# 13x13 depthwise convolutions on TensorE: column-shifted copies in the contraction, four channels in column tiles, and Toeplitz matrices expanded in DRAM early

## The chip, the cores and the metric

One core of one Trainium2 chip. The metric is the time of one execution on the device, in microseconds. All numbers in tables by stage come from the trace of one profiled execution of each kernel. A kernel that was timed in several rounds has a median and an interval; a kernel that was looked at once has one time, its state is unknown, and it is compared by its stages and not by its total.

## The reference

Four layers on a batch of 8 images, 384 channels of 32x32, fp32. Layer 0 is a norm, a scan in both directions and a gated 3x3 convolution; layer 1 is a convolution block, linear attention and an MLP. The change concerns layers 2 and 3 (cut to what matters):

```python
# layer 2: seven depthwise convolutions, each with its batch norm, summed
out = bn_eval(dwconv(x, w_lk, 1), ...)                     # 13x13
for i, (w, r) in enumerate(zip(branch_ws, (1, 1, 2, 3, 4, 5))):
    out = out + bn_eval(dwconv(x, w, r), ...)              # 5x5 to 3x3, dilated
# layer 3
y = jnp.einsum('bchw,oc->bohw', x, pw_w)                   # pointwise
x_pw = bn(y, ...) + x
out = bn(dwconv(x_pw, dwk_w), ...)                         # 13x13
out = out + bn(x_pw * dw1_w.reshape(1, -1, 1, 1), ...)
return jax.nn.gelu(out, approximate=False)
```

Both layers are one 13x13 depthwise convolution each, once the norms and small kernels are folded into it. So the end of the program is: convolution a, pointwise product, convolution b.

## The kernel before

Image rows lie in the partitions: four channels of 32 rows fill 128 partitions. For each of the 13 column shifts, one product with a 128x128 matrix that holds four 32x32 Toeplitz blocks on its diagonal does all 13 row taps of four channels. Three quarters of that matrix are zero.

```python
x2_d = dram.tile([C, H, B, W], FP, tag="x2_d", name="x2_d")   # input of convolution a
xp_d = dram.tile([C, H, B, W], FP, tag="xp_d", name="xp_d")   # input of convolution b
...
def conv(g_d, src_d, tag, put):
    srcv = src_d.rearrange("(g q) h b w -> g (q h) (b w)", q=4)
    for g in range(NG):                                    # 96 groups of four channels
        if g % GB == 0:
            xt = cxp.tile([P, GB, BW], FP, tag="xt", ...)
            nc.sync.dma_start(xt, srcv[g : g + GB].rearrange("g p n -> p g n"))
        tp = toep[g % NTO]
        for q in range(4):                                 # 32x13x32 windows, 128 B pieces
            one_k = g_d[4 * g + q]
            win = bass.AP(one_k.tensor, one_k.offset, [[1, H], [TG, KS], [1, H]])
            eng = nc.sync if q % 2 == 0 else nc.scalar
            eng.dma_start(tp[q * H : (q + 1) * H, :, q * H : (q + 1) * H], win)
        ...
        for i, kx in enumerate(order):
            s = kx - KS // 2
            lo, hi = _span(s, W)
            nc.tensor.matmul(pv[:, :, lo:hi], tp[:, kx, :], xg[:, :, lo + s : hi + s], ...)
        put(g, ps[:, 0:BW])
...
# pointwise, 16 steps t of two rows of all images
yt = cxp.tile([P, NC, NB], FP, tag="yp", ...)
nc.sync.dma_start(yt, yf[:, :, t * NB : (t + 1) * NB])
...
nc.gpsimd.dma_start(xf[:, :, t * NB : (t + 1) * NB], xo)   # 2 KB pieces
...
# the end of layer 1, image b
nc.gpsimd.dma_start(x2v[m, :, h * (H // 2) : (h + 1) * (H // 2), b, :], o...)  # 128 B pieces
```

## Time and profile before

| stage, by the first product of each (us) | start | length |
|---|---|---|
| layer 0 | 0 | 5215.2 |
| layer 1, to the first product of convolution a | 5215.2 | 2449.7 |
| convolution a | 7664.9 | 496.8 |
| pointwise | 8161.7 | 136.2 |
| convolution b, to the end of the span at 8791.0 | 8297.9 | 493.1 |

The median of four runs is 8790.78 us (8789.93 to 8792.42). The prediction below shows the lines that tell what bounds the convolutions. Two further views matter for what follows. First the DMA issues of the kernel before (written tile, read tensor, queue, count, KB each, median us from issue to landing):

```profile
x_d<-x POOLq DMA_DIRECT2D x48, 256.0 KB, 6.0
...
yp<-y_d SPq DMA_DIRECT2D x16, 768.0 KB, 5.1
xp_d<-xo POOLq DMA_DIRECT2D x16, 768.0 KB, 6.6
out<-ot POOLq DMA_DIRECT2D x96, 128.0 KB, 2.9
```

The pointwise layer's loads (yp) and stores (xp_d) land in 5 to 7 us. `x_d<-x` is the store at the end of layer 1. Both it and `out` write pieces of 128 B. Second, the pointwise stage as a stretch (start and end, us, busy us of PE, PEld, DVE, ACT, POOL with instruction counts, then granted clock, DMA share, GB/s):

```profile
8165.00:8285.00 120.00, 120.00 (x278) 53.07 (x277) 31.83 (x46) 35.74 (x46) 11.44 (x15) 0.99 0.57 182
```

TensorE is busy for all of the 120 us. This stage is bound by TensorE, and DMA is at 0.57.

### The profile page before, as it was taken

Reading aid. Unit: us, or ns where it says so; the run is one execution under the profiler, and the core shown is the slowest. Engines: PE = TensorE matmul, PEld = TensorE weight load, DVE = VectorE, ACT = ScalarE, POOL = GpSimd, SP = SyncE. Lnnn points to the kernel's source line nnn. Section 1 sums busy time; section 2 is a strip of 40 time slices with the busy share of each in tenths; the row PEclk is TensorE's granted clock in tenths of the full one; section 3 lists DMA queues with packets and bytes.
Section 4 is the critical chain, followed back from the end, with each engine's and each line's share of the span. In section 5 each row is a group of like instructions: output and inputs, shape, how many; then the busy total and the mean of one; then the engine's idle time right before and its main releaser. Section 6 shows DMA issues by size and latency. Waiting matters only on the chain.

```text
span 8791.0 us, 45960 instructions
## 1 busy us (share of the span) xinstructions
PE 6984.9 (79%) x17022; PEld 3339.6 (38%) x17022; DVE 4659.7 (53%) x3671; ACT 2213.2 (25%) x2563; POOL 269.2 (3%) x354
## 2 busy tenths in 40 slices
PE   7576676776776766767766679999899998999999
PEld 3132222222222322322322233443444344499599
DVE  2957857867767777677687972342333234100100
ACT  4333233233233233233233211111111111100100
POOL 1000000000000000000000000000000000000011
PEclk8788788788788788778878789999999999999999
DMA  2212111121121121121121220000000000144544
GB/s 69 72 60 67 65 65 65 61 70 64 57 74 64 56 75 64 56 75 64 54 70 68 72 93 11 4 15 15 11 4 15 11 7 4 25 93 95 148 95 86
DMA packets 488852, 492.32 MB, mean 56 GB/s; under 512 B 349212, under 2 KB 378036, under 8 KB 488628
## 3 DMA queue, kind: packets, MB, share of 16 engines
q1 hardware_dynamic: 295220, 382.66, 14.2%
q0 software_dynamic: 24176, 80.14, 3.1%
q10 hardware_dynamic: 169232, 26.58, 1.8%
q8 instruction: 135, 2.21, 0.1%
q14 instruction: 89, 0.73, 0.0%
HBM read 409.15 MB, written 80.11 MB: 56 GB/s over the span
## 4 chain that ended last, share of the span: by engine, by line
PE 37%; issue 32%; DVE 24%; ACT 6%; DMA 1%; POOL 1%; DVEq 0%; POOLq 0%; SPq 0%; ACTq 0%
PE acc L468 10%; DVE hs L463 9%; DVE du L458 5%; PE cv_a L244 5%; PE lc L381 4%; DVE hs L461 4%; PE c L406 4%; DVE hs L466 3%; PE cv_b L244 3%; PE in L360 2%; PE op L484 2%; ACT L435 1%; ACT L436 1%; PE mf L701 1%; PE mo L708 1%
## 5 line engine op out<-in xcount | busy, mean ns | idle before, releaser
L468 PE MATMUL acc<-hs,ident 128*128 128x512 f32 x3072 | 2224.3, 876 | 1369.6 <-DVE hs L466 1369.5
L468 PEld LDWEIGHTS acc<-hs,ident 128*128 128x128 f32 x3072 | 768.5, 269 | 2827.1 <-DVE hs L466 2024.6
L456 ACT ACTIVATE da<-dl,neg_a 128x1024 f32<-128x1024 f32 x768 | 881.1, 1148 | 2478.2 <-DVE hs L461 1298.6
L461 DVE TENSOR_TENSOR_SCAN hs<-da,du 128x1024 f32<-128x1024 f32 x384 | 875.3, 2287 | 169.0 <-PE acc L468 149.1
L466 DVE TENSOR_TENSOR hs<-hs,cc 128x1024 f32<-128x1024 f32 x768 | 919.5, 1215 | 0.4
L458 DVE TENSOR_TENSOR du<-uc,bb 128x1024 f32<-128x1024 f32 x768 | 914.3, 1210 | 0.4
L463 DVE TENSOR_TENSOR_SCAN hs<-da,du 128x1024 f32<-128x1024 f32 x384 | 877.0, 2287 | 4.3 <-PE acc L468 4.2
L701 PE MATMUL mf<-ln,wm 128*128 128x512 f32 x1152 | 562.4, 629 | 78.3 <-DVE ln L695 78.3
L714 DVE SCALAR_TENSOR_TENSOR x<-mo,pk,x 128x512 f32<-128x512 f32 x48 | 36.0, 751 | 1041.8 <-PE mo L708 1038.4
L708 PE MATMUL mo<-hm,wm 128*128 128x512 f32 x1152 | 539.7, 607 | 1.4 <-ACT hm L706 1.4
L244 PE MATMUL cv_b<-xt_b,toep 128*128 128x240 f32 (+6 forms) x2496 | 488.3, 358 | 9.6 <-DMA xt_b<-xp_d 9.6
L244 PE MATMUL cv_a<-xt_a,toep 128*128 128x240 f32 (+6 forms) x2496 | 487.4, 358 | 6.8 <-DMA toep<-g_d 6.8
L244 PEld LDWEIGHTS cv_b<-xt_b,toep 128*128 128x128 f32 x2496 | 466.4, 190 | 31.9 <-issue 10.4
L244 PEld LDWEIGHTS cv_a<-xt_a,toep 128*128 128x128 f32 x2496 | 465.8, 190 | 28.2 <-issue 6.9
L701 PEld LDWEIGHTS mf<-ln,wm 128*128 128x128 f32 x1152 | 232.5, 204 | 382.1 <-issue 282.4
L706 ACT ACTIVATE hm<-mf,biasf 128x512 f32<-128x512 f32 x192 | 131.9, 687 | 951.2 <-PE mf L701 951.2
L381 PE MATMUL lc<-xn,dg 128*128 128x496 f32 (+3 forms) x864 | 356.9, 575 | 0.0
L406 PE MATMUL c<-u,dg 128*128 128x512 f32 (+3 forms) x768 | 334.7, 595 | 5.9 <-ACT dl L434 3.1
L708 PEld LDWEIGHTS mo<-hm,wm 128*128 128x128 f32 x1152 | 205.7, 189 | 328.9 <-issue 199.0
L390 DVE TENSOR_TENSOR lg<-lg,xn 128x512 f32<-128x512 f32 x48 | 33.2, 692 | 496.5 <-ACT lg L389 496.5
L360 PE MATMUL in<-xn,win 128*128 128x512 f32 x576 | 256.4, 603 | 40.4 <-DMA win<-in_inproj_t 26.0
L448 DVE TENSOR_TENSOR uc<-uc,dl 128x1024 f32<-128x1024 f32 x48 | 58.0, 1220 | 398.9 <-PE acc L444 398.7
(153 smaller groups left out, 5628.9 us busy)
## 6 DMA issues: line engine op xcount, KB each, us to landing
bb<-bc_d SPq DMA_DIRECT2D x256, 512.0 KB, 3.6
cc<-bc_d SPq DMA_DIRECT2D x256, 512.0 KB, 3.6
toep<-g_d ACTq DMA_DIRECT2D x384, 52.0 KB, 2.7
toep<-g_d SPq DMA_DIRECT2D x384, 52.0 KB, 2.5
xn<-in_x SPq DMA_DIRECT2D x8, 1536.0 KB, 7.3
xr<-in_x SPq DMA_DIRECT2D x48, 256.0 KB, 3.2
x_d<-lg POOLq DMA_DIRECT2D x48, 256.0 KB, 3.6
fr<-x_d SPq DMA_DIRECT2D x48, 256.0 KB, 2.9
```

The source lines that it names most:

```text
L244: nc.tensor.matmul(pv[:, :, lo:hi], tp[:, kx, :], xg[:, :, lo + s : hi + s], start=(i == 0), stop=(i == KS - 1),)
L360: nc.tensor.matmul(ps, win[:, k, m * P : (m + 1) * P], xn[:, k, bass.ts(h, HALF)], start=(k == 0), stop=(k == NC - 1),)
L381: nc.tensor.matmul(pv[:, ylo - r0 : yhi - r0, xlo:xhi], dg3[:, c, k, :], img[:, ylo + dy : yhi + dy, xlo + dx : xhi + dx], start=(i == 0), ...
L406: nc.tensor.matmul(ps[:, lo - a : hi - a], dg1[:, c, k, :], u[:, c, lo + s : hi + s], start=(i == 0), stop=(i == 3),)
L456: nc.scalar.activation(da, dl[:, c, :], AF.Exp, scale=neg_a[:, c, n : n + 1])
L458: nc.vector.tensor_mul(du, uc[:, c, :], bb)
L461: nc.vector.tensor_tensor_scan(hs, da, du, 0.0, ALU.mult, ALU.add)
L463: nc.vector.tensor_tensor_scan(hs[:, ::-1], da[:, ::-1], du[:, ::-1], 0.0, ALU.mult, ALU.add)
L466: nc.vector.tensor_mul(hs, hs, cc)
L468: nc.tensor.matmul(acc[c][:, bass.ts(h, HALF)], ident, hs[:, bass.ts(h, HALF)], start=False, stop=(d == 1 and n == NST - 1),)
L701: nc.tensor.matmul(ps, wm1[:, k, f * P : (f + 1) * P], xn[:, k, :], start=(k == 0), stop=(k == NC - 1),)
L708: nc.tensor.matmul(acc[m], wm2[:, f, m * P : (m + 1) * P], hm, start=(f == 0), stop=(f == NF - 1),)
```

## The change

The intent: a product that is three quarters zeros wastes TensorE. Now the contraction's 128 partitions hold one channel four times, each copy shifted by one column, so one product does four column shifts, and four products (16 column positions, 13 of them used) make a channel. Each channel's output has 32 rows, so four channels sit side by side in four column tiles of 32. Image rows are stored with zero gaps of six columns between images, so that shifts need no clipping. The Toeplitz matrices are no longer read as windows during the convolution; 128 DMAs from DRAM to DRAM expand them during layer 0, where DMA is mostly idle.

```diff
+KP = 16
+BP = W + KS // 2
+RL = 320
+XL = 316
+CB = 16
...
-    x2_d = dram.tile([C, H, B, W], FP, tag="x2_d", name="x2_d")
+    x2_d = dram.tile([C, H, RL], FP, tag="x2_d", name="x2_d")
-    xp_d = dram.tile([C, H, B, W], FP, tag="xp_d", name="xp_d")
+    xp_d = dram.tile([C, H, RL], FP, tag="xp_d", name="xp_d")
+    e2_d = dram.tile([P, C, 4 * H], FP, tag="e2_d", name="e2_d")
+    e3_d = dram.tile([P, C, 4 * H], FP, tag="e3_d", name="e3_d")
...
+    def side(i, n):                       # called 16 times during layer 0
+        part = C // n
+        for g_d, e_d in ((g2_d, e2_d), (g3_d, e3_d)):
+            for j in range(4):
+                src = g_d[i * part]
+                win = bass.AP(
+                    src.tensor, src.offset + j * TG, [[1, H], [KP * TG, part], [4 * TG, 4], [1, H]]
+                )
+                dst = e_d[j * H : (j + 1) * H, i * part : (i + 1) * part, :]
+                nc.sync.dma_start(dst.rearrange("p c (s o) -> p c s o", o=H), win)
+        ... (zero fills of x2_d and xp_d)
...
+            for c0 in range(0, C, CB):    # convolution, chunks of 16 channels
+                xt = cxp.tile([P, CB, XL], FP, tag="xt", name=f"xt_{tag}_{c0}")
+                for j in range(4):
+                    nc.sync.dma_start(
+                        xt[j * H : (j + 1) * H, :, :],
+                        src_d[c0 : c0 + CB, :, j : j + XL].rearrange("c h n -> h c n"),
+                    )
+                tp = cxp.tile([P, CB, 4, H], FP, tag="tp", name=f"tp_{tag}_{c0}")
+                nc.scalar.dma_start(
+                    tp.rearrange("p c s o -> p c (s o)"), e_d[:, c0 : c0 + CB, :]
+                )
+                for g in range(c0 // 4, (c0 + CB) // 4):
...
+                    for s in range(4):
+                        for q in range(4):
+                            c = 4 * g + q - c0
+                            src = xt[:, c, 4 * s : 4 * s + B * BP].rearrange("p (b n) -> p b n", n=BP)
+                            nc.tensor.matmul(
+                                pv[q * H : (q + 1) * H], tp[:, c, s, :], src[:, :, 0:W],
+                                start=(s == 0), stop=(s == 3),
+                            )
...
-            nc.gpsimd.dma_start(xf[:, :, t * NB : (t + 1) * NB], xo)
+            rows = NB // BW
+            for m in range(NC):
+                for r in range(rows):
+                    nc.gpsimd.dma_start(
+                        xf[m, :, t * rows + r, KS // 2 : KS // 2 + B * BP].rearrange(
+                            "p (b n) -> p b n", n=BP
+                        )[:, :, 0:W],
+                        xo[:, m, r * BW : (r + 1) * BW].rearrange("p (b w) -> p b w", w=W),
+                    )
...
-                        x2v[m, :, h * (H // 2) : (h + 1) * (H // 2), b, :],
+                        x2v[
+                            m, :, h * (H // 2) : (h + 1) * (H // 2),
+                            KS // 2 + BP * b : KS // 2 + BP * b + W,
+                        ],
```

More of the change, by code (lines that the diff above doesn't have):

```diff
@@ L89, in tile_layers @@
     x1_d = dram.tile([B, C, L], FP, tag="x1_d", name="x1_d")
-    x2_d = dram.tile([C, H, B, W], FP, tag="x2_d", name="x2_d")
+    assert KS // 2 + B * BP <= RL and 3 + XL <= RL
+    x2_d = dram.tile([C, H, RL], FP, tag="x2_d", name="x2_d")
     y2_d = dram.tile([C, H, B, W], FP, tag="y2_d", name="y2_d")
-    xp_d = dram.tile([C, H, B, W], FP, tag="xp_d", name="xp_d")
-    g2_d = dram.tile([C, KS, TG], FP, tag="g2_d", name="g2_d")
-    g3_d = dram.tile([C, KS, TG], FP, tag="g3_d", name="g3_d")
+    xp_d = dram.tile([C, H, RL], FP, tag="xp_d", name="xp_d")
+    g2_d = dram.tile([C, KP, TG], FP, tag="g2_d", name="g2_d")
+    g3_d = dram.tile([C, KP, TG], FP, tag="g3_d", name="g3_d")
+    e2_d = dram.tile([P, C, 4 * H], FP, tag="e2_d", name="e2_d")
+    e3_d = dram.tile([P, C, 4 * H], FP, tag="e3_d", name="e3_d")
     bias_d = dram.tile([C], FP, tag="bias_d", name="bias_d")
@@ L154, in tile_layers @@
         nc.scalar.dma_start(k3, dwk.rearrange("(c p) k -> p c k", p=P))
-        g2 = kern.tile([P, NC, KS, TG], FP, tag="g2", name="g2")
+        g2 = kern.tile([P, NC, KP, TG], FP, tag="g2", name="g2")
         nc.gpsimd.memset(g2, 0.0)
-        g3 = kern.tile([P, NC, KS, TG], FP, tag="g3", name="g3")
+        g3 = kern.tile([P, NC, KP, TG], FP, tag="g3", name="g3")
         nc.gpsimd.memset(g3, 0.0)
@@ L175, in tile_layers @@
             src = k3[:, c, :].rearrange("p (a b) -> p a b", b=KS)
-            nc.vector.tensor_scalar_mul(g3[:, c, :, off : off + KS], src, bns("dwk", c))
+            nc.vector.tensor_scalar_mul(g3[:, c, 0:KS, off : off + KS], src, bns("dwk", c))
             mid = g3[:, c, KS // 2, off + KS // 2 : off + KS // 2 + 1]
@@ L185, in tile_layers @@
             nc.gpsimd.dma_start(biasq_d, bias_d.rearrange("(g q) -> q g", q=4))
-    _layer0(tc, nc, B, xv, x1_d, dram, ident, mean_w, eps6, one, vec, neg_a, rs, rsm,
+    zero = const.tile([P, 4 * RL], FP, tag="zero", name="zero")
+    nc.gpsimd.memset(zero, 0.0)
+    def side(i, n):
[8 more added lines that the diff above has]
+                nc.sync.dma_start(dst.rearrange("p c (s o) -> p c s o", o=H), win)
+        rows = H // 8
+        if i % (n // 8) == 0:
+            r = i // (n // 8) * rows
+            for d in (x2_d, xp_d):
+                for c in range(NC):
+                    nc.sync.dma_start(
+                        d[c * P : (c + 1) * P, r : r + rows, :].rearrange("p h n -> p (h n)"), zero
+                    )
+    _layer0(tc, nc, B, xv, x1_d, dram, side, ident, mean_w, eps6, one, vec, neg_a, rs, rsm,
             inproj_t, xproj_t, dtproj_t, outproj_t)
@@ L197, in tile_layers @@
     ) as cps:
-        NTO = 4
-        toep = []
-        for i in range(NTO):
-            t = cwp.tile([P, KS, P], FP, tag=f"toep{i}", name=f"toep{i}")
-            nc.gpsimd.memset(t, 0.0)
-            toep.append(t)
         pwt = cwp.tile([P, NC, C], FP, tag="pwt", name="pwt")
@@ L221, in tile_layers @@
             nc.vector.tensor_add(pbias[:, m, :], pbias[:, m, :], bias2[:, m, :])
-        def conv(g_d, src_d, tag, put):
-            srcv = src_d.rearrange("(g q) h b w -> g (q h) (b w)", q=4)
-            order = [KS // 2] + [i for i in range(KS) if i != KS // 2]
-            xt = None
-            for g in range(NG):
-                if g % GB == 0:
-                    xt = cxp.tile([P, GB, BW], FP, tag="xt", name=f"xt_{tag}_{g}")
-                    nc.sync.dma_start(xt, srcv[g : g + GB].rearrange("g p n -> p g n"))
-                tp = toep[g % NTO]
-                for q in range(4):
-                    one_k = g_d[4 * g + q]
-                    win = bass.AP(one_k.tensor, one_k.offset, [[1, H], [TG, KS], [1, H]])
-                    eng = nc.sync if q % 2 == 0 else nc.scalar
-                    eng.dma_start(tp[q * H : (q + 1) * H, :, q * H : (q + 1) * H], win)
-                ps = cps.tile([P, HALF], FP, tag="cv", name=f"cv_{tag}_{g}")
-                pv = ps[:, 0:BW].rearrange("p (b w) -> p b w", w=W)
-                xg = xt[:, g % GB, :].rearrange("p (b w) -> p b w", w=W)
-                for i, kx in enumerate(order):
-                    s = kx - KS // 2
-                    lo, hi = _span(s, W)
-                    nc.tensor.matmul(
-                        pv[:, :, lo:hi], tp[:, kx, :], xg[:, :, lo + s : hi + s],
-                        start=(i == 0), stop=(i == KS - 1),
-                    )
-                put(g, ps[:, 0:BW])
@@ new lines, in conv @@
+        def conv(e_d, src_d, tag, put):
+            for c0 in range(0, C, CB):
+                xt = cxp.tile([P, CB, XL], FP, tag="xt", name=f"xt_{tag}_{c0}")
+                for j in range(4):
+                    nc.sync.dma_start(
+                        xt[j * H : (j + 1) * H, :, :],
+                        src_d[c0 : c0 + CB, :, j : j + XL].rearrange("c h n -> h c n"),
+                    )
+                tp = cxp.tile([P, CB, 4, H], FP, tag="tp", name=f"tp_{tag}_{c0}")
[3 more added lines that the diff above has]
+                for g in range(c0 // 4, (c0 + CB) // 4):
+                    ps = cps.tile([P, HALF], FP, tag="cv", name=f"cv_{tag}_{g}")
+                    pv = ps[:, 0:BW].rearrange("p (b w) -> p b w", w=W)
+                    for s in range(4):
[6 more added lines that the diff above has]
+                            )
+                    put(g, ps[:, 0:BW])
@@ L261, in put2 @@
                 nc.gpsimd.dma_start(y2v[g - GB + 1 : g + 1].rearrange("g p n -> p g n"), hold["t"])
-        conv(g2_d, x2_d, "a", put2)
+        conv(e2_d, x2_d, "a", put2)
         yf = y2_d.rearrange("(k p) h b w -> p k (h b w)", p=P)
-        xf = xp_d.rearrange("(k p) h b w -> p k (h b w)", p=P)
+        xf = xp_d.rearrange("(k p) h n -> k p h n", p=P)
         NB = min(HALF, H * BW)
@@ L292, in put3, with _layer0 @@
             )
-        conv(g3_d, xp_d, "b", put3)
-def _layer0(tc, nc, B, xv, x1_d, dram, ident, mean_w, eps6, one, vec, neg_a, rs, rsm,
+        conv(e3_d, xp_d, "b", put3)
+def _layer0(tc, nc, B, xv, x1_d, dram, side, ident, mean_w, eps6, one, vec, neg_a, rs, rsm,
             inproj_t, xproj_t, dtproj_t, outproj_t):
@@ L495, in _layer0 @@
             bwd = direction(b, 1, u)
+            side(2 * b, 2 * B)
             scan(b, 0, *fwd, acc)
+            side(2 * b + 1, 2 * B)
             if b + 1 < B:
@@ L515, in _layer1 @@
         x1v = x1_d.rearrange("b (c p) l -> b p c l", p=P)
-        x2v = x2_d.rearrange("(c p) h b w -> c p h b w", p=P)
+        x2v = x2_d.rearrange("(c p) h n -> c p h n", p=P)
         def psum(name):
```

## The prediction

> **What bounds the kernel now.** I read the page first: the slices give the stages. Columns are 40 slices of 220 us; a digit is the busy share in tenths.
>
> ```profile
> PE   7576676776776766767766679999899998999999
> DVE  2957857867767777677687972342333234100100
> PEclk8788788788788788778878789999999999999999
> DMA  2212111121121121121121220000000000144544
> ```
>
> Up to slice 23 (layer 0) DVE and PE share the work, the scan being DVE's; slices 24 to 34 (layer 1) are TensorE; the last five are the two 13x13 convolutions with a pointwise layer between. Only there does DMA reach 4 to 5 tenths. The change speeds up these five slices and puts new transfers into the first 23. Next, the groups of the convolutions, by line (busy us, mean ns, idle before):
>
> ```profile
> L244 PE MATMUL cv_b<-xt_b,toep 128*128 128x240 f32 (+6 forms) x2496 | 488.3, 358 | 9.6 <-DMA xt_b<-xp_d 9.6
> L244 PE MATMUL cv_a<-xt_a,toep 128*128 128x240 f32 (+6 forms) x2496 | 487.4, 358 | 6.8 <-DMA toep<-g_d 6.8
> L244 PEld LDWEIGHTS cv_a<-xt_a,toep 128*128 128x128 f32 x2496 | 465.8, 190 | 28.2 <-issue 6.9
> ```
>
> Each convolution is 487 to 488 us of TensorE with next to no waiting. 96 groups x 13 products are 1248, yet the row counts 2496: an fp32 product is two instructions, each with its own weight load. 487.4 / 2496 is 195 ns start to start (the 358 ns include the pipeline). A group is 26 x 195 ns = 5.08 us; the 13 shifts have 2992 columns together, so a column costs 5.08 us / (2 x 2992) = 0.85 ns per pass. Then the stretches (PE, PEld, DVE, ACT, POOL busy; clock, DMA share, GB/s), in steady convolution and in the steady scan:
>
> ```profile
> 7700.00:8100.00 400.00, 400.00 (x2059) 382.69 (x2059) 16.96 (x40) 14.51 (x39) 15.05 (x20) 1.00 0.45 95
> 2850.00:2990.00 140.00, 93.12 (x112) 35.29 (x112) 124.25 (x83) 30.66 (x28) 0.00 (x0) 0.66 0.22 71
> ```
>
> In the convolution TensorE is busy 400 of 400 us at clock 1.00: **TensorE bound**, DMA under half used. In the scan DVE is busy 124 of 140 us and DMA has 78% to spare. Last, the DMA queues over 7700 to 8100:
>
> ```profile
> q1 hardware_dynamic: 78816, 18.91, 24.5%
> q10 hardware_dynamic: 68256, 8.42, 13.9%
> ```
>
> q10 carries almost only Toeplitz windows in 128 B packets: 13.9% x 16 engines x 400 us / 68256 is 13.0 ns per packet, 9.8 GB/s per engine. In the first 7 us of the pointwise loads (2 KB packets, 128 partitions) I get 20.7 GB/s per engine, and the same (20.8) from the first xt_b loads with 1 KB packets. The only transfer worth reading on 32 partitions is the store of B and C: 0.13 MB, 28.6% of 16 engines in a 2 us window, 14.3 GB/s per engine.
>
> **What the Trainium skill says.** (1) "TensorEngine Tiling (Array Packing)", Tiling Modes: different tiles can load weights and multiply in parallel, four of them at 128x32. No run here shows it yet: every convolution row above is 128*128. (2) "TensorE: Matmul & The Clock Gate", Part 3: three column tiles gave 2.38x; matmuls start and end strictly in order. The trace shows neither. (3) "SBUF — State Buffer", Door 1: partitions 0..31 reach 8 of 16 DMA ports, 189 GB/s at 1 MiB against 328 for all 128. The 14.3 against 20.8 GB/s per engine point the same way (229 against 333 GB/s over 16 engines), on one small store. (4) "DMA: Bandwidth & Descriptors", Specifications: line rate needs 512 B or more. The trace agrees: 9.8 GB/s per engine at 128 B, 20.8 at 1 KB.
>
> **The change, part by part.**
>
> *Convolution, TensorE.* 13 products of 128x128 per group become 16 of 128x32 (4 row-shift blocks x 4 channels, the channels in adjacent column tiles), each over all 256 columns. One pass is 256 x 0.85 = 217 ns. With no overlap of tiles a group is 32 x 217 ns = 6.9 us, worse than 5.08. With ideal overlap of four it would be 1.7 us. I expect between: the two passes of one product use the same tile and come one after the other; in strict order the second pass of channel q can overlap only the first pass of channel q+1, so one channel costs one pass: 16 x 217 ns = **3.5 us per group**, 13.9 us per chunk of 16 channels.
>
> *Convolution, DMA.* Per chunk (24 per convolution): xt is now loaded four times, shifted by one pixel, in four DMAs of 32 partitions x 16 x 1264 B, together 2.59 MB instead of 0.52. At 229 GB/s: 11.3 us. tp is 128 rows of 8 KB, 1.05 MB at 333 GB/s: 3.1 us. The y store, 0.52 MB: 1.6 us. Sum **16.0 us per chunk**, more than TensorE's 13.9. In the second convolution the output store takes the place of y (q0 over 8320 to 8760: 18.2 GB/s per engine, 0.52 MB, 1.8 us): 16.2 us. The 128 B windows, 768 DMAs, are gone from here. The new bound is thus the load of the shifted copies. The order of instructions keeps two chunks of prefetch: the tp load of chunk k+2 stands on ACT's queue right after the evictions of chunk k. Allowing 0.5 us per chunk for imperfect overlap, the convolutions take 24 x 16.5 = 396 and 24 x 16.8 = 403 us: **-91 and -85 us**.
>
> *Starts.* The first chunk needs 2.6 MB instead of 0.5 before the first product: about 11.3 + 2.2 us after issue. Before, it was 9 us for the first convolution and 4 us for the second: **+5 and +10 us**.
>
> *Pointwise layer.* Its output goes out in 96 stores of 1024 pieces of 128 B, not 16 of 2 KB pieces. Such stores exist already (out, same size): 886 ns of POOL each. Six per step are 5.3 us, and a step takes 7.7 us of TensorE (18 instructions x 0.43 us). Hidden: 0.
>
> *Layer 0.* 128 DRAM-to-DRAM DMAs of 3072 pieces of 128 B expand the matrices: at 13 ns on 16 engines 2.5 us each, 320 us in all, and 48 zero fills of 640 KB at 333 GB/s are 2 us each, 94 us. All stand on SP's queue among the loads of B and C. Have these room? From the queue's and DVE's timeline (start, us):
>
> ```profile
> 2883.30 0.32 SPq L451 DMA_DIRECT2D bb<-bc_d  x1
> ```
>
> ```profile
> 2902.39 2.35 DVE L458 TENSOR_TENSOR du<-uc,bb 128x1024 f32<-128x1024 f32 x2
> ```
>
> The product that needs this bb starts 19.1 us after its issue, and bb lands in 3.6: about 15 us of slack. The built order puts mostly one expansion, at times three, or six zero fills, between two loads: 2.5 to 12 us. Mostly hidden; I allow **+20 us** for scan starts, where loads follow B and C directly, and for a somewhat different interleaving.
>
> *Layer 1.* Same stores with another row pitch: 0.
>
> Sum: 8790.5 - 91 - 85 + 5 + 10 + 20 = **8650 us**, 1.6% less.
>
> **The rivals.**
> (a) *Column tiles do not overlap for fp32.* Then TensorE needs 27.7 us per chunk, 665 us per convolution: 2 x 177 more, 9180 us. Against it speaks the skill's 2.38x; for it, that nothing in this trace uses tiles and that fp32 doubles each product. I give it 13%.
> (b) *The loads run at full port rate.* Then 2.59 MB take 7.8 us, a chunk 12.5 us of DMA, and TensorE's 13.9 us bounds it: about 14.3 us per chunk, 343 us per convolution, some 8540 us. For it: 128-partition loads do reach 333, and loads on even and odd ports might overlap. If tiles also overlapped better than I think, DMA at 12.5 would give about 8460. 35% for this direction.
> (c) *The 128 B DRAM-to-DRAM writes are slow.* The 13 ns are from DRAM to SBUF. At 80 ns a DMA would take 15 us, the slack would be gone, and SP, in order, would hold up B and C: hundreds of us in layer 0, 8900 or more. The x2 stores of 128 B pieces (2048 pieces, 6.0 us to landing) argue against more than some 30 ns. 7%.
> (d) *Waiting cools the clock.* With gaps of 2 us per chunk the granted clock could fall as in the scan (0.66) and TensorE would need more than its 13.9 us: up to 18 us per chunk, 8720 us. It lies inside the range.
>
> **Range and chances.** The centre is 8650. The low end, 8510, is (b) with most of its gain; the high end, 8880, is slower loads (18 us per chunk) with 150 us of harm in layer 0. 2% faster means below 8615, only 35 us under the centre, about 1 us per chunk: so faster 0.37. Within 2%, up to 8966: 0.47. Slower, which is (a) or a bad (c): 0.16.
>
> **What would show it right or wrong.** Right: the convolution rows are 128*32, x3072 each; one starts about every 108 ns on average while running; TensorE waits at chunk starts for xt; the DMA digits of the last slices are 8 or 9, at 215 to 230 GB/s; each convolution spans 380 to 420 us; DVE in layer 0 has next to no wait for bb or cc, and layer 1 begins within 40 us of where it did. Wrong: starts 217 ns apart (rival a); xt moving at 300 GB/s (b); DVE waiting for bb after expansions that take over 10 us to land (c); a clock well below 0.9 in the convolutions (d). The prediction fails most easily on the rate of 32-partition loads, which rests on one small store, and on the overlap of tiles, which rests on no run of this case.

## The result, and the profile after

The changed kernel's median is 8759.94 us (four runs, 8755.63 to 8763.78), against 8790.78 us before. The ratio is 0.9965, with a 95% interval of 0.9951 to 0.9979. Ratios here are the mean time of one kernel's fast runs over that of the other's from the same rounds, so not quite the ratio of the medians. A gain of 141 us was forecast, and 31 us came.

By stage, from the traces (us):

| stage | before | after | change | the prediction's terms |
|---|---|---|---|---|
| layer 0 | 5215.2 | 5176.6 | -38.6 | +20 |
| layer 1, to first product of a | 2449.7 | 2465.2 | +15.5 | +5 |
| convolution a | 496.8 | 398.6 | -98.2 | -91 |
| pointwise, to first product of b | 136.2 | 321.8 | **+185.6** | 0 + 10 |
| convolution b, to the end | 493.1 | 398.2 | -94.9 | -85 |
| sum | | | -30.6 | -141 |

The convolutions gave what was forecast. The pointwise stage, where the arithmetic is the same instruction for instruction, became 2.4 times as long. It shows in the 40 slices of the page of the kernel after (219 us each; the stage fills slice 38):

```profile
PE   7576676776767767867856679989999998855545
DMA  5333433333121121121121220101001010299999
GB/s 109 112 94 103 112 105 106 100 97 101 64 75 64 62 70 64 57 75 62 48 79 66 72 86 11 8 11 15 11 4 15 13 6 4 59 252 201 77 218 234
```

The last five slices have DMA at 9 everywhere and TensorE at 4 or 5 tenths, so the bound has moved from TensorE to DMA. But read the two lines together: in slice 38 DMA is just as busy as in its neighbours and moves only 77 GB/s, against 201 to 252. Busy, yet moving a third: these transfers are slow in themselves. The first ten slices show the expansions, with DMA at 3 to 5 where it was 1 or 2.

The groups on the same page (busy us, mean ns, idle before and what ended it):

```profile
L272 PE MATMUL cv_b<-xt_b,tp_b 128*32 128x256 f32 x3072 | 225.6, 463 | 207.7 <-DMA xt_b<-xp_d 178.2
...
L272 PE MATMUL cv_a<-xt_a,tp_a 128*32 128x256 f32 x3072 | 222.6, 460 | 186.0 <-DMA xt_a<-x_d 150.8
...
L303 PE MATMUL pw<-yp,pwt 128*128 128x512 f32 x288 | 147.2, 674 | 146.7 <-DMA yp<-y_d 146.7
```

Each convolution has 223 to 226 us of TensorE and waits another 151 to 178 us for xt. The pointwise products wait 146.7 us for their loads. The DMA issues of the kernel after:

```profile
e_d<-g_d SPq DMA_DIRECT2D x128, 384.0 KB, 6.1
...
x_d<-x POOLq DMA_DIRECT2D x48, 256.0 KB, 12.8
...
yp<-y_d SPq DMA_DIRECT2D x16, 768.0 KB, 39.5
xp_d<-xo POOLq DMA_DIRECT2D x96, 128.0 KB, 23.7
```

The pointwise loads are untouched by the change, yet they land in 39.5 us instead of 5.1. The stores of 128 KB take 23.7 us where 768 KB took 6.6. The layer-1 stores, the same 256 KB in the same 128 B pieces, have gone from 6.0 to 12.8 us. The loads are the victims and the stores the suspects. The waits of the kernel after in its pointwise stage, 8030 to 8365 us (engine and line, what it waited for, us in total, times, longest):

```profile
PE pw L303 <- DMA yp<-y_d: 146.7, 11, 26.9
POOL xp_d L314 <- DMA xp_d<-xo: 145.1, 60, 7.0
```

GpSimd itself waits for its own earlier stores before it can issue the next. The queue of these stores over 8040 to 8340 us (packets, MB, share of 16 engines), and then the stretches of convolution a and of the pointwise stage, all of the kernel after:

```profile
q0 software_dynamic: 4562, 12.48, 63.6%
```

```profile
7700.00:8000.00 300.00, 169.38 (x2304) 93.70 (x2304) 15.28 (x36) 13.41 (x36) 13.55 (x18) 0.74 1.09 252
8050.00:8340.00 290.00, 137.60 (x270) 57.66 (x268) 31.80 (x46) 35.38 (x46) 82.30 (x93) 0.75 0.96 78
```

q0 carries these stores: 63.6% of 16 engines for 300 us is 3053 us of engine time for 96 x 1024 = 98,304 pieces, 31 ns a piece. The `out` stores in convolution b, pieces of the same 128 B, came to 627 us for 89,088 pieces, 7 ns a piece. The extra 24 ns x 98,304 / 16 engines is 147 us, about four fifths of the 185.6 us that the stage lost. The packets of the loads beside them became slower too: 31.1% of the same 300 us, 1493 us for 11.55 MB, against 647 us for 10.23 MB in the stretch of 120 us before. That is an estimated 48 us more on each of 16 engines. So the question is what makes one 128 B piece four times as dear as another.

### The profile page after: what moved, and what is told of

It reads as the page before. It is cut to its first block, busy times and chain, and to the rows that moved or that the text cites. A ratio compares the mean times of both kernels' runs of the same rounds, so it can differ in the third digit from the quotient of the medians.

```text
span 8760.4 us, 47408 instructions
## 1 busy us (share of the span) xinstructions
PE 6425.3 (73%) x18174; PEld 2632.0 (30%) x18174; DVE 4654.9 (53%) x3671; ACT 2216.4 (25%) x2565; POOL 338.8 (4%) x431
## 4 chain that ended last, share of the span: by engine, by line
issue 34%; PE 27%; DVE 26%; DMA 6%; ACT 6%; POOL 2%; SPq 0%; another core or an unknown queue 0%; DVEq 0%; POOLq 0%; ACTq 0%
DVE hs L499 9%; PE acc L504 8%; DVE du L494 6%; DVE hs L497 5%; PE lc L417 4%; PE c L442 3%; DVE hs L502 3%; DMA xt_a<-x_d 3%; PE in L396 3%; DMA xp_d<-xo 2%; PE op L520 2%; ACT L471 1%; ACT L472 1%; PE mf L739 1%; PE cv_a L272 1%
## 5 line engine op out<-in xcount | busy, mean ns | idle before, releaser
L504 PE MATMUL acc<-hs,ident 128*128 128x512 f32 x3072 | 2169.5, 853 | 1383.7 <-DVE hs L502 1383.7
L504 PEld LDWEIGHTS acc<-hs,ident 128*128 128x128 f32 x3072 | 734.7, 259 | 2815.5 <-DVE hs L502 2082.0
L272 PE MATMUL cv_b<-xt_b,tp_b 128*32 128x256 f32 x3072 | 225.6, 463 | 207.7 <-DMA xt_b<-xp_d 178.2
L272 PE MATMUL cv_a<-xt_a,tp_a 128*32 128x256 f32 x3072 | 222.6, 460 | 186.0 <-DMA xt_a<-x_d 150.8
L303 PE MATMUL pw<-yp,pwt 128*128 128x512 f32 x288 | 147.2, 674 | 146.7 <-DMA yp<-y_d 146.7
L661 PE MATMUL kv<-wqkv,xx 128*128 128x384 f32 x768 | 249.0, 486 | 0.0
## 6 DMA issues: line engine op xcount, KB each, us to landing
tp_b<-e_d ACTq DMA_DIRECT2D x24, 1024.0 KB, 12.2
```

What stands on the lines that cost most here:

```text
L272: nc.tensor.matmul(pv[q * H : (q + 1) * H], tp[:, c, s, :], src[:, :, 0:W], start=(s == 0), stop=(s == 3),)
L504: nc.tensor.matmul(acc[c][:, bass.ts(h, HALF)], ident, hs[:, bass.ts(h, HALF)], start=False, stop=(d == 1 and n == NST - 1),)
```

## The experiments

Twelve kernels ran, each with runs of the kernel before on the same chip. Unless a line says otherwise a kernel's result was correct.

### Why the pointwise stage grew

**pw_rows: whole rows instead of pieces.** xo holds full rows of 320 with zero gaps, written once, and is stored as in the kernel before, 16 stores of 2560 B pieces.

```diff
-            for m in range(NC):
-                for r in range(rows):
-                    nc.gpsimd.dma_start(xf[m, :, t * rows + r, KS // 2 : ...][:, :, 0:W], xo[:, m, ...])
+            nc.gpsimd.dma_start(
+                xf[:, :, t * rows : (t + 1) * rows, :].rearrange("k p h n -> p k (h n)"),
+                xo.rearrange("p k h n -> p k (h n)"),
+            )
```

> One part of the changed kernel undone: the pointwise layer stores whole padded rows (1280 B, zeros included, from an SBUF tile kept padded) in 16 stores instead of 96 stores of 128 B pieces. All else as changed. Theory (the 128 B pieces that start off any 64 B boundary are what makes the pointwise stage 322 us instead of 136): the stage, from its first product to the first product of the second convolution, falls to 140-155 us, the stores land in 4-8 us, and the kernel takes 8570-8600 us. Rival (the stage is slow because of the wide pitch of the padded layout, 40960 B between the channels that one store spreads over): the pitch stays, so the stage stays above 250 us.

Measured, three rounds: 8587.05 us (8586.73 to 8588.23), ratio to before 0.9768 (0.9752 to 0.9785). The pointwise stage, to the first product of b, took 147.1 us instead of 321.8. The issues of pw_rows, its stores and the loads beside them:

```profile
xp_d<-xo POOLq DMA_DIRECT2D x16, 960.0 KB, 7.7
...
yp<-y_d SPq DMA_DIRECT2D x16, 768.0 KB, 5.8
```

The stores are the cause: with whole rows the loads are back to 5.8 us. But this edit changes the size of the pieces, their number, their starts and the number of DMAs at once.

**aligned48 and shifted48: where a piece starts.** Two layouts with the same pitch of 48 columns per image and rows of 416 (1664 B), the same 96 stores of 128 B pieces. They differ only in the first column: 16 (pieces start at byte 64 + 192 b) or 6 (24 + 192 b, as the first image of the changed kernel). Neighbouring pieces are 64 B apart in both, so no two share a block of 32 B.

```diff
-BP = W + KS // 2
-RL = 320
-XL = 316
+BP = 48
+OFF = 16          # aligned48; 6 in shifted48
+RL = 416
+XL = 396
-  src_d[c0 : c0 + CB, :, j : j + XL]
+  src_d[c0 : c0 + CB, :, OFF - KS // 2 + j : OFF - KS // 2 + j + XL]
-  KS // 2 : KS // 2 + B * BP          (and KS // 2 + BP * b in layer 1)
+  OFF : OFF + B * BP                  (and OFF + BP * b)
```

> Changed kernel with images 48 columns apart and 16 columns of lead, so that every 128 B piece starts on a 64 B boundary; still 96 stores of 1024 pieces. The convolutions' loads grow from 1264 to 1584 B rows, so only the pointwise stage is compared. Theory (pieces off the 64 B boundary): the stage falls from 322 to 140-180 us. Rival 1 (any 128 B piece with gaps around it is slow): it stays at 280 us or more. Rival 2 (issue on GpSimd): stays.

> As the run with 48 columns between images, but with 6 columns of lead, so that pieces start 24 B past a 64 B boundary and no two pieces share a 64 B block. Theory A (a piece off its boundary is slow by itself): the pointwise stage is again 280 us or more, and the stores of layer 1 land in about 12 us as in the changed kernel. Theory B (slow only because neighbouring pieces write into the same 64 B block): it is 140-180 us as with aligned pieces.

Measured, one look each: the pointwise stage took 146.1 us in aligned48 and 353.5 us in shifted48 (totals 8739.92 and 8963.58 us; both load 25% more into xt than the changed kernel, which costs their convolutions). Issues of aligned48:

```profile
x_d<-x POOLq DMA_DIRECT2D x48, 256.0 KB, 6.0
yp<-y_d SPq DMA_DIRECT2D x16, 768.0 KB, 5.3
xp_d<-xo POOLq DMA_DIRECT2D x96, 128.0 KB, 4.7
```

Issues of shifted48:

```profile
x_d<-x POOLq DMA_DIRECT2D x48, 256.0 KB, 14.4
yp<-y_d SPq DMA_DIRECT2D x16, 768.0 KB, 51.3
xp_d<-xo POOLq DMA_DIRECT2D x96, 128.0 KB, 25.6
```

Same count, size, pitch, queue and neighbours; only the start differs, and the stores land in 4.7 or in 25.6 us. It is neither the piece size nor the 96 DMAs nor their issue: aligned48 still issues 96 of them and its stage is as short as that of pw_rows. Over 8125 to 8265 us, aligned48's stores took 42.0% of 16 engines: 941 us for the same 98,304 pieces, 9.6 ns a piece instead of 31.

**hw_stores: another queue.** The 96 stores of the changed kernel are issued by SP and not by GpSimd.

```diff
-                    nc.gpsimd.dma_start(
+                    nc.sync.dma_start(
                         xf[m, :, t * rows + r, KS // 2 : KS // 2 + B * BP].rearrange(
```

> Changed kernel with the 96 stores of the pointwise layer issued by SP instead of GpSimd. Theory (cost lies in the writes to DRAM): the stage stays within 15% of 322 us. Rival (GpSimd's descriptors or its queue are the limit): it falls below 200 us.

Measured, one look: 8772.9 us, stage 340.9 us. The issue of its stores:

```profile
xp_d<-xo SPq DMA_DIRECT2D x96, 128.0 KB, 15.2
```

A store lands earlier after its issue, but the stage is no shorter. GpSimd's wait of 145 us was a symptom.

**How fine is the boundary?** The changed kernel holds an experiment of its own. In layer 1 it stores image b at byte 24 + 152 b of a row of 1280 B. By image, the stores' median landing was 15.2, 14.9, 15.1, **6.5**, 15.0, 15.2, 14.7 and **6.2** us. The starts modulo 32 are 24, 16, 8, **0**, 24, 16, 8 and **0**. Here are image 2 (start at byte 328) and image 3 (byte 480, which is 32 over a multiple of 64), issues of the kernel after in two windows:

```profile
x_d<-x POOLq DMA_DIRECT2D x6, 256.0 KB, 15.1
```

```profile
x_d<-x POOLq DMA_DIRECT2D x6, 256.0 KB, 6.5
```

Only two images of eight are fast. Starts on a multiple of 16 alone (images 1 and 5) are slow, and image 3 is fast off a 64 B boundary: this says 32 B. To have it in the pointwise stage too, **aligned32** uses a pitch of 40 columns from column 8 and rows of 344 (1376 B), so pieces start at 32 + 160 b; every start is a multiple of 32 and half of them are not multiples of 64.

```diff
-BP = 48           # aligned48
-OFF = 16
-RL = 416
-XL = 396
+BP = 40
+OFF = 8
+RL = 344
+XL = 332
```

> The changed kernel with images 40 columns apart, starting at column 8: the same 96 pointwise stores of 128 B pieces, now starting at byte 32 + 160 b of a row whose pitch is 1376 B (43 times 32), so every piece starts on a 32 B boundary and half of them off a 64 B one. Theory (the cost is that of a write that starts off a 32 B boundary): the pointwise stage takes 140 to 155 us, its stores land in 4 to 6 us, and the layer-1 stores of all eight images land in 5.5 to 7 us. Rival (the boundary that matters is 64 B): half the pieces stay slow, the stage takes over 200 us, and the layer-1 stores land in 10 us or more. Time by the theory about 8600 to 8680 us (loads 5% larger than in the changed kernel).

Measured, one look: the stage took 143.7 us, and the layer-1 stores landed in 5.9 to 6.0 us for images 0 to 6 (7.6 in the last window, which holds three stores). Its issues and its pointwise stretch:

```profile
x_d<-x POOLq DMA_DIRECT2D x48, 256.0 KB, 6.0
...
xp_d<-xo POOLq DMA_DIRECT2D x96, 128.0 KB, 4.8
```

```profile
8005.00:8145.00 140.00, 125.50 (x288) 55.05 (x287) 33.25 (x48) 37.30 (x48) 84.62 (x96) 0.95 0.83 189
```

Granularity of 32 B is thus shown twice. GpSimd is busy 85 of 140 us with issuing the 96 stores, and that is indeed hidden, as was forecast. The total, 8559.92 us, was below what was expected; the stages say why: layer 0 ended 48 us earlier than in the changed kernel (see the last experiment). What happens inside the DMA engines at such a write, such as a read of the block's rest, is not shown; only its price is.

### What bounds the convolutions now

The forecast was 16.0 us of DMA per chunk; 386 us from first to last product of convolution a, over 24 chunks, is 16.1. The rate of the 32-partition loads was its weak point, so three runs took it up. All three are pw_rows with a further edit. The baseline, pw_rows over 7700 to 7950 us (packets, MB, share):

```profile
q1 hardware_dynamic: 31959, 39.18, 80.1%
```

80.1% x 16 x 250 us is 3204 us of engine time for 39.18 MB: 12.2 GB/s per engine, 196 over all 16. (These rates count only the time in which a queue's packets are under way, and the shares of several queues can add up to over 100%. Over all queues and the whole window, pw_rows moved 254 GB/s.)

**unshifted: are the loads slow because they start off a boundary too?** All four copies read from column 0. The result is wrong on purpose (relative error 1.09).

```diff
-                        src_d[c0 : c0 + CB, :, j : j + XL].rearrange("c h n -> h c n"),
+                        src_d[c0 : c0 + CB, :, 0:XL].rearrange("c h n -> h c n"),
```

> Wrong result on purpose: whole-row stores, all four copies of a chunk loaded from the unshifted address, so that every 1264 B row starts on a 256 B boundary; same bytes, still 32 partitions per DMA. Theory (the 32 partitions are the limit, not the odd start of the reads): convolutions within 3% of 385 and 400 us. Rival (reads that start off a boundary cost, as the writes do): both fall below 350 us.

Measured, one look: convolution a took 383.5 us from first to last product, and in pw_rows 384.9. So these reads, whose shifted copies start 4 to 12 B later, pay nothing that shows for it, while the writes do. Other starts and sizes of reads were not tried.

**wide_load: one DMA of 128 partitions, as many bytes.** Wrong on purpose (relative error 1.16).

```diff
-                for j in range(4):
-                    nc.sync.dma_start(xt[j * H : (j + 1) * H, :, :], src_d[...])
+                base = src_d[min(c0, C - CB - 4)]
+                nc.sync.dma_start(
+                    xt, bass.AP(base.tensor, base.offset, [[RL, P], [H * RL, CB], [1, XL]])
+                )
```

> Wrong result on purpose: whole-row stores, and each chunk's xt loaded by one DMA over 128 partitions from consecutive rows, with the same bytes in the same 1264 B rows, all starting on a 256 B boundary. Theory (32 partitions per DMA are the limit): xt moves at about 330 GB/s instead of 194, a chunk takes 12-13 us, a convolution about 300 us, the kernel about 8400 us. Rival (1264 B packets themselves are slow): as before, 385-400 us per convolution.

Measured, one look: convolution a took 318.3 us from first to last product and b 281.4, where pw_rows had 384.9 and 399.5. The queue of wide_load in the same window:

```profile
q1 hardware_dynamic: 36634, 45.94, 53.7%
```

That is 21.4 GB/s per engine, 342 over 16. The narrow loads cost nearly half of this rate.

**two_queues: the copies on two queues.** Copies 0 and 1 (partitions 0 to 63) stay on SP with tp, copies 2 and 3 (64 to 127) go to ACT. The result is correct.

```diff
-                    nc.sync.dma_start(
+                    (nc.sync if j < 2 else nc.scalar).dma_start(
                         xt[j * H : (j + 1) * H, :, :],
...
-                nc.scalar.dma_start(
+                nc.sync.dma_start(
                     tp.rearrange("p c s o -> p c (s o)"), e_d[:, c0 : c0 + CB, :]
```

> Whole-row stores as in the first experiment (8587 us), and the four shifted copies of a chunk split over two queues: copies 0 and 1 (partitions 0 to 63) on SP with the matrices, copies 2 and 3 (partitions 64 to 127) on ACT. Same bytes. Theory (the loads are slow because each DMA reaches 32 partitions and so half of the SBUF ports; two at once on different halves fill all ports): a chunk falls from 16.1 to 12.5-14 us, each convolution from 385-400 to 300-340 us, the kernel to 8420-8500 us. Rival (the rate is bound elsewhere, by the packets or by reading DRAM, or DMAs on the two halves do not run together): within 1% of 8587 us.

The SBUF ports of this expectation are those of the prediction's point (3); no trace here shows ports.

Measured, three rounds: **8447.15 us** (8439.55 to 8452.17), ratio to before 0.9606 (0.9591 to 0.9620), the fastest of all versions that are right. Convolution a took 319.6 us from first to last product, b 333.8. Its two load queues in the same window:

```profile
q1 hardware_dynamic: 21167, 42.83, 55.2%
q10 hardware_dynamic: 18414, 22.57, 28.6%
```

65.4 MB in 83.8% of 16 engines x 250 us: 19.5 GB/s per engine, 312 in all, against 196 for xt on one queue. Over all queues the core moved 301 GB/s in this window, against 254 in pw_rows. So loads to different halves of the partitions do run beside each other when they stand on two queues. That it takes different halves, and not just two queues, is not shown: no run puts copies of the same half on two queues, and the edit also moves tp to SP.

**best: two_queues with a third xt and tp buffer, and without the fill of xp_d** that whole rows make needless.

```diff
-            for d in (x2_d, xp_d):
+            for d in (x2_d,):
...
-    xt = cxp.tile([P, CB, XL], FP, tag="xt", ...)   # and tp
+    xt = cxp.tile([P, CB, XL], FP, tag="xt", ..., bufs=3)
```

> Whole-row stores, the copies on two queues (8447 us), three buffers instead of two for copies and matrices, and no zero fill of the fourth layer's input, which the whole rows now write. Theory (with two buffers DMA still pauses, busy 0.94; a third fills the pauses): a chunk falls from 13.4 to 12.3-13 us, the kernel to 8390-8430 us. Rival (the transfers themselves are the limit): 8435-8455 us.

Measured, three rounds: 8513.76 us (8502.73 to 8519.17), ratio 0.9682 (0.9666 to 0.9698), which is 67 us slower than two_queues and a miss for both theories. Layer 1 begins at 5171.7 us, against 5171.0 in two_queues, so the missing fills do nothing that shows. The convolutions are longer: 357.2 and 365.9 us from first to last product. SP's loads landed in 25.3 us and ACT's in 16.4, with DMA busier than in two_queues and moving 274 GB/s instead of 308. That the two queues fall out of step when they may run further ahead, and so land on the same half, would fit; it was not tested and stays open.

### Do column tiles overlap in fp32?

The forecast had 3.5 us per group by the argument that the two passes of an fp32 product use the same tile and only neighbours overlap. Two runs of the changed kernel with another order of its 16 products per group test it.

**same_tile**: the four products of one channel (one tile) in a row.

```diff
-                    for s in range(4):
-                        for q in range(4):
+                    for q in range(4):
+                        for s in range(4):
```

> Changed kernel with the two inner loops exchanged: the four products of one channel, all in one column tile, follow one another, and the tiles come in turn. Same products, same loads. If the four tiles work at once only when products for different tiles stand next to each other in order (theory), a group takes up to 6.9 us at the full clock instead of 1.7, a chunk 21-28 us, and a convolution 500-665 us instead of 386-393. Rival (the order of products does not matter, or the array packs them anyway): the convolutions stay at 386-393 us.

**pair_tiles**: two tiles in turn, then the other two.

```diff
-                    for s in range(4):
-                        for q in range(4):
+                    for qq, s, q in [(qq, s, qq + i) for qq in (0, 2) for s in range(4) for i in range(2)]:
```

> Changed kernel with only two column tiles in turn: channels 0 and 1 alternate over the four blocks, then channels 2 and 3. Measured is the time from one group's eviction to the next inside a chunk at the full clock: 1.70 us with four tiles in turn, 3.55 us with the products of a tile together. Theory (a pass over 256 columns takes 0.107 us in a 32-column tile, and in strict order the second pass of a product overlaps only the first pass of the next one): two tiles in turn suffice, a group takes 1.7-1.8 us. Rival (a pass takes 0.21 us and all four tiles run at once): with two tiles in turn the group takes about 3.5 us.

Measured, one look each (8898.3 and 8791.95 us). ACT and DVE evict every second group each, so two evictions of one engine within a chunk are two groups apart. The timeline of ACT after (start, us, what), then of DVE in same_tile and in pair_tiles:

```profile
7826.22 0.37 ACT L285 COPY yt<-cv_a 128x256 f32<-128x256 f32 x1 [10.15 <-PE cv_a L272]
7829.63 0.37 ACT L285 COPY yt<-cv_a 128x256 f32<-128x256 f32 x1 [3.04 <-PE cv_a L272]
```

```profile
7825.80 0.42 DVE L287 COPY yt<-cv_a 128x256 f32<-128x256 f32 x1 [15.79 <-PE cv_a L272]
7832.89 0.42 DVE L287 COPY yt<-cv_a 128x256 f32<-128x256 f32 x1 [6.67 <-PE cv_a L272]
```

```profile
7823.46 0.42 DVE L287 COPY yt<-cv_a 128x256 f32<-128x256 f32 x1 [6.44 <-PE cv_a L272]
7827.01 0.42 DVE L287 COPY yt<-cv_a 128x256 f32<-128x256 f32 x1 [3.12 <-PE cv_a L272]
```

A group takes 3.41 / 2 = 1.70 us with four tiles in turn, 3.55 / 2 = 1.78 with two, and 7.09 / 2 = 3.55 with one. So two tiles in turn give nearly all there is, a factor of 2.0, and four hardly more, 2.1. Convolution a of same_tile took 442.6 us from first to last product: less than its theory expected (500 to 665 us) and more than its rival (386 to 393), a miss for both.

The group times fit the theory of pair_tiles: a pass takes 0.107 us and overlaps only its neighbour. The starts of the passes in the traces (each pass is one MATMUL instruction; read over 6 to 12 us of convolution a) do not. In the kernel before they come one at a time, 215 to 216 ns apart at 256 columns. In same_tile two start within 31 ns, and such pairs follow each other every 216 to 247 ns. In pair_tiles and in the changed kernel four start within 19 to 45 ns, and such fours follow every 216 to 254 ns. So two passes start together in one tile, which the forecast's argument rules out, and the step is still the 0.217 us that it took for one pass. What fits both times and starts is a pass of the forecast's length, with two at once in one tile and four at once in two or more tiles. How long a pass lasts is not shown, since the profile models its end; nor is what stops at four.

### What the added transfers do to layer 0

**before_side: the kernel before, with only the expansions and zero fills added.** They go into DRAM that nothing reads; the kernels' columns in DRAM are padded to 16, as in the change.

```diff
+    def side(i, n): ...                    (as in the change; fills go to z2_d, zp_d)
...
             bwd = direction(b, 1, u)
+            side(2 * b, 2 * B)
             scan(b, 0, *fwd, acc)
+            side(2 * b + 1, 2 * B)
```

> Kernel before plus the 128 expansions and 48 zero fills among the loads of layer 0, results unused, all else as before. The changed kernel began layer 1 39 us earlier than the kernel before. Theory (these transfers, placed by the scheduler, shift the order of the work in layer 0, and this is the gain): layer 1 begins 25-45 us earlier and the kernel takes 8745-8765 us. Rival (the gain is from something else, and the transfers cost time): 8790-8830 us.

Measured, three rounds: 8751.1 us (8746.02 to 8757.72), ratio 0.9950 (0.9933 to 0.9967). The first products of layer 1 in before, after and before_side:

```profile
L586 PE MATMUL h<-xx,c x288: 592/592/1201, 5215.2 to 7360.2; 128*128 128x512 f32 x144
```

```profile
L624 PE MATMUL h<-xx,c x288: 592/592/1201, 5176.6 to 7321.7; 128*128 128x512 f32 x144
```

```profile
L617 PE MATMUL h<-xx,c x288: 592/592/1201, 5180.0 to 7325.3; 128*128 128x512 f32 x144
```

The added transfers alone bring layer 1 forward by 35 us, and the rest of before_side is as before. From one image's first scan to the next image's, the trace after has 613, 661, 640 and 621 us and then 645 three times; before it was 641 and then 645 six times. So the gain lies where the expansions run (the last is issued at 2137.6 us). What the other order does for it is not settled. The nine kernels with the same layer 0 as the changed kernel (best with half of the fills) began layer 1 between 5166.5 and 5176.6 us. Those with larger fills began it at 5128.7 (aligned32), 5186.4 (aligned48) and 5194.3 us (shifted48), in no order of size. So a difference of this kind in layer 0 should not be read as an effect of an edit elsewhere.

## Why the prediction was right or wrong

- **The step that failed is "Pointwise layer. ... Hidden: 0."** It counted GpSimd's time to issue 96 stores, 886 ns each, which was right (85 us of a 140 us stage in aligned32, hidden). It took the `out` stores as the model ("Such stores exist already (out, same size)") and never asked where the pieces start. `out` pieces start on multiples of 128 B, these at 24 + 152 b. The runs put +185.6 us in the place of 0 + 10, and aligned48 against shifted48 takes it away by the start alone (146.1 against 353.5 us).
- **"Layer 1. Same stores with another row pitch: 0"** is the same error: these stores went from 6.0 to about 15 us for six of eight images. It cost no time that shows: the last image is one of the two with aligned starts, and its last store landed in 6.1 us in both kernels before convolution a's loads were issued.
- **"Starts ... +5"** was too small: that stage became 15.5 us longer. From the issue of convolution a's first xt load to its first product it is 24.7 us after, against 9.1 before; the forecast had 11.3 + 2.2.
- **The convolutions' DMA was right**: 16.0 us per chunk forecast, 16.1 measured, though by two errors that cancel. The rate was 196 GB/s where one small store had suggested 229, so xt alone takes 13.2 us and not 11.3. In return tp and y move partly beside it: the shares of the three queues of pw_rows in that window (80.1, 19.6 and 8.2%) add up to 108%. DMA is the bound. -98.2 and -94.9 us came where -91 and -85 were forecast. Part of this is luck, by the next point.
- **The TensorE term failed too**: 3.5 us per group forecast, 1.70 measured. The step that failed is that "the two passes of one product use the same tile and come one after the other": in same_tile two passes start together in one tile. The 217 ns held as the step between starts. Nor would the forecast's 13.9 us per chunk have been hidden behind 16 us of DMA: same_tile has it (4 x 3.55 = 14.2 us) with the same loads, and its convolution a took 442.6 us, not 396. Over 7700 to 8000 us its loads waited 164.9 us for products to free their buffers, and DMA moved 223 GB/s; in the changed kernel it was 96.5 us and 252 GB/s. So the forecast for the convolutions came true only with a TensorE twice as fast as it assumed.
- **Rival (a)**, no overlap, is out: a group takes 1.70 us with four tiles in turn and 3.55 with one. **Rival (b)**, loads at the full rate, is not what the changed kernel does, but two_queues shows that it was to be had for an edit of two lines: 312 GB/s. **Rival (c)** named the danger, slow writes of 128 B pieces, but in the wrong place. It spoke of the expansions, which landed in 6.1 us rather than the 2.5 of transfer assumed and did no harm. It was then dismissed with the layer-1 stores of the kernel before, which are aligned. **Rival (d)**, a cooler clock, came (0.74 in the convolutions); no cost of it shows, as TensorE waits for xt there.
- **Layer 0** was forecast +20 and came out -38.6, the wrong sign. before_side shows that it comes from the added transfers; the reason is open.

So one term of 176 us, outside the part that the change was about, took up most of the gain.

## What to carry to other kernels

When a layout gets gaps, check the byte at which each written piece starts: choose offset and pitch as multiples of 32 B, or write whole rows with the gaps in them. A slice with DMA at nine tenths and few GB/s was the mark of such transfers here, and the loads beside them looked guilty when the stores were the cause. When loads fill 32 partitions each, try those for different halves of the partitions on different queues before counting on their rate. And when a sum comes out right, check its terms: here the terms of the convolutions were wrong and offset one another.

## What the Trainium skill lacked or had wrong

- **What a write to DRAM that starts off a 32 B boundary costs** is in no page. Only "Collectives: The Full Stack", section Rules for kernel authors, asks for 32-byte aligned buffers, to prevent a read-modify-write, and it gives no cost. "DMA: Bandwidth & Descriptors", section Specifications, has 512 B as the least size for line rate, with read-modify-write below it. Here size did not decide: 128 B pieces took about 7 ns (`out`, aligned), 9.6 ns (aligned48) or 31 ns (unaligned), and the stage with aligned 128 B pieces (146.1 us) was as short as with 2560 B rows (147.1 us).
- **"SBUF — State Buffer", section "Can I just issue two DMAs to hit both halves?"**, says no: +6%, they serialize. In two_queues, loads to the two halves from two queues went at 312 GB/s while under way, against 196 on one queue; the whole core moved 301 GB/s against 254, and the convolutions became 65 us shorter each. Its section on Door 1 was borne out: 196 GB/s for 32 partitions and 342 for 128 while under way (the page, for 1 MiB: 189 and 328).
- **"TensorEngine Tiling (Array Packing)", Tiling Modes**, has tiles running in parallel, and does not say what fp32's two passes do to it: two tiles in turn gave 2.0 (3.55 to 1.78 us per group), four gave 2.1. Within one tile, two passes started together every 216 to 247 ns.
